# Attention with a graph dilation beside it: small numbers on GpSimd, one comparison moved between two products, second projections in another bank, and joined statistics

## The chip, the core and the metric

The kernel runs on one core of a Trainium2 chip. The metric is the device time of one launch in microseconds: 3422.03 us before the change, the median of three runs (3410.63 to 3422.94). The profiled execution took 3413.46 us, of which 3411.7 us lie between its first and its last instruction.

In the profile PE is TensorE's matmuls, PEld its weight loads, DVE VectorE, ACT ScalarE, POOL GpSimd and SP SyncE. Times are microseconds unless marked ns.

## What is computed

There are 16 graphs with 1024 nodes each and 128 features per node. Two layers follow each other.

```python
h = relu(layernorm(x))
x = x + attention(h, adj)          # 8 heads of 16, masked where adj == 0, weighted by adj
h = relu(layernorm(x))
x = x + sage(h, dilate(adj))       # three SAGE layers with batch norms, a projection at the end

# attention, per graph and head
scores = q @ k.T / sqrt(16);  scores[adj == 0] = -inf
attn = softmax(scores) * adj;  attn = attn / (attn.sum(-1) + 1e-8);  ctx = attn @ v

# dilate, per graph: rows in their order, each row sees what earlier rows removed
for n in range(1024):
    num = row.sum()
    sf = (num + 1) // 2 if num > 10 else 1
    removed = row & (cumsum(row) % sf == 0)      # if num > 1
    row n and column n lose what is removed
```

A row with more than ten neighbours loses the neighbour whose rank is sf and the one whose rank is twice sf; a row with two to ten loses all. The dilation needs only the adjacency, so it can run beside the attention.

## The kernel before

`swept` has two stages. The first (`first_part`) runs the attention of all graphs, the layer norms and, beside them, the dilation. The second runs the three SAGE layers. The change touches the first stage alone.

**The attention** (`attention`, L527) goes through 256 turns: graph b, half c of the query columns (512 of them), block m of 128 keys. Each turn has two half-steps, g = 0 and 1, with four heads each. A half-step gives VectorE, ScalarE and TensorE this work:

- `scores` (L586): 16 small bf16 matmuls that put a large negative number where there is no edge (L601), then the products of q and k (L609), into two PSUM tiles `sc` of two banks each.
- Two exponentials on ScalarE (L643), each over 128x1024: tiles `e`.
- Two products on VectorE (L658): `w` is `e` times the transposed adjacency `aT`, 128x1024 f32 each. These are the two weighted exponentials.
- `values` (L531): the sums with v (L534, from `w`) and the denominators' part (L539, from `e`), issued one half-step late.
- Once per turn, `turn_over` (L544): TensorE transposes the adjacency block two turns ahead into PSUM bank `m` (L552), ScalarE evicts it (L555) and makes the mask (L559), and SP sends it away.

**What is woven in.** Preparations of the next graph (`prepare`: layer norm, transposes, projections to q, k and v), conclusions of the last one (`conclude`) and the like are generators. They lie in the list `beside`; at marked places of a half-step `go_on_with(kind)` lets one whose last yield named that kind go on. `both_groups` (L352) is the generator of the q and k projections: for each of two groups a matmul of 512 columns into a PSUM tile (L356), an eviction by ScalarE (L337, L345) and a second one by VectorE that keeps the low part (L339, L347). All four of a graph's projections use the one PSUM bank `m` for both groups (graph 0's first two alternate with bank `d`). So the second group's matmul comes after VectorE has read the first, and when the second group is still to be read, `held` is true (L632) and the transposes of `turn_over`, which need bank `m` too, are issued later.

**The layer norms** (`layer_norm_relu`, L288) take `bn_stats` per block of 128 nodes (L294: for each half of the features count, mean and count times variance), join the two halves with `bn_aggr` (L296), raise the variance to the power -1/2 on GpSimd (L302) and let ScalarE apply scale and bias (L308). There are 32 of them over eight blocks, the first in two parts.

**The dilation** (`dilation`, L708) goes through eight blocks k of 128 rows, all 16 graphs at once, rows on partitions. Per block:

1. VectorE builds prefix sums `w` of the diagonal blocks by scans (L813) and the masks `up`, `valid`, `final`. The small numbers of 128x16 (`onw`, `total`, `most`, `half`, `end16`, L831 to L843) say how many neighbours a row has and where its middle is.
2. Seven rounds (L863 on) find a fixed point. A round takes `gone`, what the other rows removed, from PSUM bank `d`. From it come `num` and `y`, then `c`, `high` and `at16` (L880, L881, L884), all of 128x16. Then `hit` compares the 128x2048 prefix sums with `at16` (L893), and TensorE counts the hits per row into `gone` (L899, 16 matmuls of one column). Rounds in the set `full` also make `vb` (L887 to L891) and 32 more matmuls (L903, L904). `full` has two of the seven rounds in blocks 0 to 4, four in block 5, and all in blocks 6 and 7: 28 of 56.
3. The last numbers (L911 to L922), the removal from the diagonal blocks (L925 to L937), then 18 iterations over the graphs that apply the result to all columns: scan (L957), transposes (L964), evictions (L966), comparisons (L973 to L992) and the reading of the next block.

**What sets the order.** `beside_attention` (L1006) is a planner written out by hand. `dilation` is a generator that yields a cost in us and when it wants to go on: 0 at once, 1 after the next half-step, "A" or "B" at the next half-step of that parity. After each half-step the planner takes steps of the dilation while the costs spent lie below a share of the total that grows with the half-steps; the total is made of the cost of a block, in which a round counts 2.5. A yield marked "counts" makes the planner issue the scores of the next half-step before the dilation goes on, so that the matmuls of `gone` stand behind these scores in TensorE's queue. Rounds 1 and 3 wait one half-step between the small numbers and `hit`.

```python
                    yield (1.6 if r in full else 1.0), (1 if r in (1, 3) else 0)
                    nc.vector.tensor_tensor(in_pairs(hit), in_pairs(w), over_rows(at16), ALU.is_equal)
                    yield 1.3, 1, "counts"
```

Each engine works through its instructions in the order in which they are issued here, with small moves by a scheduler. GpSimd's queue holds little before the change: the powers of the layer norms (L302), casts of reciprocals (L457), the fill of `go_on` (L803), and DMAs.

## Time and profile before

| | PE | PEld | DVE | ACT | POOL |
|---|---|---|---|---|---|
| busy us | 3238.2 | 1904.3 | 3050.6 | 2350.6 | 165.4 |
| share of the span | 95% | 56% | 89% | 69% | 5% |
| instructions | 34987 | 34987 | 5410 | 3942 | 253 |

| costliest rows of the first stage | count | busy us | mean ns |
|---|---|---|---|
| L658 DVE, products `w` | 1024 | 1210.7 | 1219 |
| L643 ACT, exponentials `e` | 1024 | 997.6 | 1022 |
| L534 PE, sums with v | 4096 | 605.2 | 608 |
| L539 PE, denominators | 4096 | 587.1 | 593 |
| L609 PE, scores | 4096 | 378.9 | 444 |

The profiled execution took 3413.46 us and its span is 3411.7 us; 1.8 us lie around it. Busy time is a union of intervals from start to end of each instruction; instructions that follow each other on an engine overlap a little, so the distance from start to start is the better price. PE's ends are modelled, and a busy PE isn't PE at its peak. The chain that ended last holds only the last two VectorE instructions in this trace, so what bounds the kernel has to be read from stretches, groups and timelines. A wait is given with what ended it ("<-ACT e L643").

### The profile page before, as it was taken

The page shows a single profiled execution, that of the slowest core. Times are in us where ns is not written, and L with a number is a line of the kernel's source. Part 1 is how long each engine was busy: PE and PEld are TensorE (multiplying, and loading weights), DVE is VectorE, ACT ScalarE, POOL GpSimd, SP SyncE. Part 2 cuts the span into 40 slices and gives each one's busy share as a digit, 9 for nine tenths or more (in the row PEclk, how much of TensorE's full clock was granted, in tenths as well). Part 3 has the DMA queues.
Part 4 walks back from the last instruction along what each step waited for, and adds up shares of the span by engine and source line. Part 5 has one row for each costly group of instructions (what it writes and reads, how often), then busy time and mean ns, then how long its engine had stood idle before and what let it go on. Part 6 is the DMA issues. An engine that isn't in the chain of part 4 may idle for free. (4 is left out here: it accounts for less than half of the span.)

```text
span 3411.7 us, 86821 instructions
## 1 busy us (share of the span) xinstructions
PE 3238.2 (95%) x34987; PEld 1904.3 (56%) x34987; DVE 3050.6 (89%) x5410; ACT 2350.6 (69%) x3942; POOL 165.4 (5%) x253
## 2 busy tenths in 40 slices
PE   8999999999999999999899999999999899999997
PEld 3433333333343333333334334346999899999997
DVE  7988988998999898998999999997888799988887
ACT  7699789779879979978987996994322344433324
POOL 2000000000000000000000010001000000000000
PEclk9999999999999999999999999999999999999999
DMA  7356456547646746754864783577999799989996
GB/s 237 108 168 197 138 147 204 153 133 214 183 127 200 226 125 181 236 152 146 240 190 127 221 256 105 167 241 268 347 343 341 284 350 351 349 326 350 352 348 223
DMA packets 650126, 772.31 MB, mean 226 GB/s; under 512 B 173264, under 2 KB 569168, under 8 KB 637424
## 3 DMA queue, kind: packets, MB, share of 16 engines
q1 hardware_dynamic: 632672, 708.58, 64.1%
q0 software_dynamic: 15456, 57.30, 4.8%
q8 instruction: 276, 4.52, 0.6%
q14 instruction: 138, 1.13, 0.1%
q10 hardware_dynamic: 1584, 0.79, 0.1%
HBM read 508.50 MB, written 157.29 MB: 195 GB/s over the span
## 5 line engine op out<-in xcount | busy, mean ns | idle before, releaser
L658 DVE TENSOR_TENSOR w<-e,aT 128x1024 f32<-128x1024 f32 x1024 | 1210.7, 1219 | 139.6 <-ACT e L643 138.0
L643 ACT ACTIVATE e<-sc 128x1024 f32<-128x1024 f32 x1024 | 997.6, 1022 | 194.1 <-PE sc L609 193.0
L1196 PE MATMUL pg<-y,aT 128*128 128x128 f32 (+1 forms) x6144 | 730.6, 275 | 0.0
L1196 PEld LDWEIGHTS pg<-y,aT 128*128 128x128 f32 x6144 | 708.7, 192 | 0.0
L534 PE MATMUL acc<-w,both 128*32 128x512 f32 x4096 | 605.2, 608 | 3.5 <-DVE w L658 1.9
L539 PE MATMUL acc<-e,eps 128*32 128x512 f32 x4096 | 587.1, 593 | 0.0
L147 DVE SCALAR_TENSOR_TENSOR aT<-mr,aT 128x1024 f32<-128x1024 bf16 x384 | 458.8, 1217 | 0.0
L609 PE MATMUL sc<-q,k 32*128 32x512 f32 x4096 | 378.9, 444 | 0.0
L601 PE MATMUL sc<-nomask,never 32*32 32x512 bf16 x8192 | 287.8, 384 | 70.2 <-ACT e L643 62.9
L601 PEld LDWEIGHTS <-never 32*32 32x32 bf16 x8192 | 91.3, 87 | 412.9 <-issue 392.7
L539 PEld LDWEIGHTS acc<-e,eps 128*32 128x32 f32 x4096 | 152.4, 110 | 298.3 <-issue 291.2
L1219 ACT ACTIVATE sq<-o 128x512 f32<-128x512 f32 x96 | 60.6, 631 | 328.4 <-DVE o L1214 328.4
L1237 ACT COPY hT<-pt 128x512 f32<-128x512 f32 x96 | 56.2, 585 | 288.5 <-PE pt L1233 280.0
L609 PEld LDWEIGHTS sc<-q,k 32*128 32x128 f32 x4096 | 155.3, 183 | 150.1 <-issue 150.0
L973 ACT ACTIVATE pair<-both,th 128x512 f16<-128x512 f16 x256 | 205.4, 881 | 2.0 <-DVE both L957 2.0
L552 PE MATMUL pa<-ident,a 128*128 128x128 f32 x1024 | 168.3, 287 | 35.1 <-DVE q L339 15.4
L534 PEld LDWEIGHTS acc<-w,both 128*32 128x32 f32 x4096 | 94.8, 108 | 181.1 <-DVE w L658 80.9
L552 PEld LDWEIGHTS pa<-ident,a 128*128 128x128 f32 x1024 | 107.6, 141 | 151.8 <-issue 61.4
L555 ACT COPY aT<-pa 128x512 f32<-128x512 f32 x256 | 152.5, 596 | 52.0 <-PE pa L552 51.4
L559 ACT ACTIVATE nomask<-aT 128x512 bf16<-128x512 f32 x256 | 161.5, 631 | 8.1
L1214 DVE SCALAR_TENSOR_TENSOR o<-pg,rdeg,mine 128x128 f32<-128x128 f32 x384 | 108.1, 344 | 56.7 <-PE pg L1196 53.5
L957 DVE TENSOR_TENSOR_SCAN both<-rk 128x513 f16<-128x513 bf16 x128 | 156.0, 1218 | 0.0
(240 smaller groups left out, 4058.2 us busy)
## 6 DMA issues: line engine op xcount, KB each, us to landing
aT<-aT_d SPq DMA_DIRECT2D x94, 2048.0 KB, 10.0
mr<-mr_d SPq DMA_DIRECT2D x188, 512.0 KB, 6.0
aT_d<-aT SPq DMA_DIRECT2D x256, 256.0 KB, 4.1
a<-in_adj SPq DMA_DIRECT2D x253, 256.0 KB, 3.4
ad<-in_adj SPq DMA_DIRECT2D x112, 512.0 KB, 4.5
nomask<-nomask SPq DMA_DIRECT2D x512, 96.0 KB, 2.7
nomask<-nomask SPq DMA_DIRECT2D x512, 64.0 KB, 2.7
nomask<-nomask SPq DMA_DIRECT2D x512, 32.0 KB, 2.6
```

The lines of the kernel that those rows point to most:

```text
L147: nc.vector.scalar_tensor_tensor(part, mrs[h][:, j : j + 2, :].rearrange("p j n -> p (j n)"), 0.0, part, ALU.is_equal, ALU.mult)
L534: nc.tensor.matmul(acc[g][32 * j : 32 * j + 32, :], v1[:, m, (2 * j + g) * HW : (2 * j + g) * HW + 32], ws[j // 2][:, j % 2, :], start=(m ...
L539: nc.tensor.matmul(acc[g][32 * j : 32 * j + 32, :], eps8, es[j // 2][:, j % 2, :], start=False, stop=(m == NB - 1),)
L552: nc.tensor.transpose(pa[:, k * P : (k + 1) * P], a[:, k, :], ident)
L559: nc.scalar.activation(nomask[:, 0, :], aT[:, 0, :], AF.Relu, bias=1.0, scale=-1e38, accum_out=zeros[:, i : i + 1])
L601: nc.tensor.matmul(scs[j // 2][to : to + 32, j % 2, :], never[rows, rows], nomask[rows, j, :], start=True, stop=False, tile_position=(32 * ...
L609: nc.tensor.matmul(scs[j // 2][:, j % 2, :], ks[m // HB][rows, g, mm], qs[c][rows, g, half, :], start=False, stop=(half == 1), tile_positi ...
L643: nc.scalar.activation(e, scs[q], AF.Exp, scale=1.0 / math.sqrt(HD))
L658: nc.vector.tensor_tensor(w, es[q], aT.to_broadcast([P, 2, HN]), ALU.mult)
L957: nc.vector.tensor_tensor_scan(pair_sums[b % 2], row[:, 0::2], row[:, 1::2], 0.0, ALU.add, ALU.add)
L973: nc.scalar.activation(wrs[b][:, t::2], pair_sums[b % 2][:, t : t + HN], AF.Abs, bias=at[:, b : b + 1], scale=2.0,)
L1196: nc.tensor.matmul(pg[:, i // 2, at : at + width], aT[:, j, i * P : (i + 1) * P], y[:, j, :width], start=(j == 0), stop=(j == NB - 1),)
```

## The change

It has four parts.

1. **Joined statistics.** `bn_aggr` goes. Six VectorE instructions on all blocks at once join the halves: difference of the means, sum of the variances, the square of the difference scaled, their sum, the scaling with epsilon, the sum of the means.
2. **Second projections in the dilation's bank.** A flag `taken["d"]` says whether a tile of bank `d` is still to be read by VectorE in the written order. If not, the second group of a projection goes to bank `d`, else to `m` as before. `held` is true only if it went to `m`.
3. **Small numbers on GpSimd.** In `dilation` the 128x16 instructions that don't read PSUM are issued on GpSimd. Where VectorE did two operations with two tensors in one instruction, GpSimd gets two instructions. `num`, `y`, `mosts` and `mids` of rounds 1 to 6 read `gone` in PSUM and stay on VectorE.
4. **The comparison between the two products.** A round's `hit` is not issued in `dilation` but put in the list `amid`, and the next half-step issues it between its two products `w`. A round yields once instead of twice, so each round takes one half-step. In the planner a round counts 1.9 instead of 2.5.

```diff
@@ layer_norm_relu
-                for j in range(i, i + 2):
-                    nc.vector.bn_aggr(mv[:, j, :], st[:, j, :])
...
-            nc.vector.tensor_scalar(rs[:, 1, n], mv[:, n, 1], LN_EPS, None, ALU.add)
+            apart, squares = mv[:, n, 0], mv[:, n, 1]
+            nc.vector.tensor_tensor(apart, st[:, n, 1], st[:, n, 4], ALU.subtract)
+            nc.vector.tensor_tensor(squares, st[:, n, 2], st[:, n, 5], ALU.add)
+            nc.vector.scalar_tensor_tensor(apart, apart, D / 4.0, apart, ALU.mult, ALU.mult)
+            nc.vector.tensor_tensor(squares, squares, apart, ALU.add)
+            nc.vector.tensor_scalar(rs[:, 1, n], squares, 1.0 / D, LN_EPS, ALU.mult, ALU.add)
+            nc.vector.tensor_tensor(apart, st[:, n, 1], st[:, n, 4], ALU.add)
             nc.gpsimd.tensor_tensor(rs[:, 0, n], rs[:, 1, n], minus_half[:, n], ALU.pow)
...
@@ both_groups
                     where, tag = banks[g % len(banks)]
+                    if g == 1 and len(banks) == 1:
+                        if not taken["d"]:
+                            where, tag = ps_d, "d"
+                        taken["m"] = tag == "m"
@@ attention
-                    held = go_on_with("next step")
+                    held = go_on_with("next step") and taken["m"]
...
                         ws.append(w)
+                        while q == 0 and amid:
+                            amid.pop()()
                         if q == 0:
                             go_on_with("low")
@@ dilation, before the rounds
-                        nc.vector.tensor_scalar(onw, w[:, :, P - 1], 1024.0, None, ALU.subtract)
+                        nc.gpsimd.tensor_scalar(onw, w[:, :, P - 1], 1024.0, None, ALU.subtract)
...
-                        nc.vector.tensor_tensor(total, left, right, ALU.add)
+                        nc.gpsimd.tensor_tensor(total, left, right, ALU.add)
...
+                    taken["d"] = True
                     yield (2.5 if c == 0 else 1.4), 1
                     nc.vector.tensor_tensor(valid[:, hb, :], pd, up[:, hb, :], ALU.mult)
+                    taken["d"] = False
...
@@ dilation, a round
+                    taken["d"] = False
                     if r == ROUNDS - 1:
-                        nc.vector.tensor_copy(prev, num)
-                    nc.vector.tensor_scalar(c, y, MAGIC, MAGIC - 5120.0, ALU.add, ALU.subtract)
-                    nc.vector.tensor_scalar(high, num, 10.5, None, ALU.is_gt)
+                        nc.gpsimd.tensor_copy(prev, num)
+                    nc.gpsimd.tensor_scalar(c, y, MAGIC, MAGIC - 5120.0, ALU.add, ALU.subtract)
+                    nc.gpsimd.tensor_scalar(high, num, 10.5, -4096.0, ALU.is_gt, ALU.mult)
...
-                    nc.vector.scalar_tensor_tensor(at16, twice(high), -4096.0, twice(c), ALU.mult, ALU.add)
+                    nc.gpsimd.tensor_tensor(at16, twice(high), twice(c), ALU.add)
                     if r in full:
...
-                        nc.vector.scalar_tensor_tensor(
-                            vb[:, 0], twice(num), 1.5, twice(high), ALU.is_gt, ALU.subtract
-                        )
-                        nc.vector.scalar_tensor_tensor(c, y, 5120.0, c, ALU.add, ALU.is_gt)
-                        nc.vector.tensor_tensor(vb[:, 1], twice(c), twice(high), ALU.mult)
-                    yield (1.6 if r in full else 1.0), (1 if r in (1, 3) else 0)
-                    nc.vector.tensor_tensor(in_pairs(hit), in_pairs(w), over_rows(at16), ALU.is_equal)
-                    yield 1.3, 1, "counts"
+                        nc.gpsimd.tensor_scalar(high, num, 10.5, None, ALU.is_gt)
+                        nc.gpsimd.tensor_scalar(lost, num, 1.5, None, ALU.is_gt)
+                        nc.gpsimd.tensor_tensor(vb[:, 0], twice(lost), twice(high), ALU.subtract)
+                        nc.gpsimd.tensor_tensor(c, y, c, ALU.subtract)
+                        nc.gpsimd.tensor_scalar(c, c, -5120.0, None, ALU.is_gt)
+                        nc.gpsimd.tensor_tensor(vb[:, 1], twice(c), twice(high), ALU.mult)
+                    amid.append(
+                        partial(nc.vector.tensor_tensor, in_pairs(hit), in_pairs(w), over_rows(at16), ALU.is_equal)
+                    )
+                    taken["d"] = True
+                    yield (2.0 if r in full else 1.7), 1, "counts"
+                    while amid:
+                        amid.pop()()
...
@@ dilation, after the rounds
                 nc.vector.tensor_tensor(changed[:, k * B : (k + 1) * B], num, prev, ALU.not_equal)
-                nc.vector.tensor_scalar(high, num, 10.5, None, ALU.is_gt)
-                nc.vector.scalar_tensor_tensor(allof, num, 1.5, high, ALU.is_gt, ALU.subtract)
+                nc.gpsimd.tensor_scalar(high, num, 10.5, None, ALU.is_gt)
+                nc.gpsimd.tensor_scalar(allof, num, 1.5, None, ALU.is_gt)
+                nc.gpsimd.tensor_tensor(allof, allof, high, ALU.subtract)
...
@@ beside_attention
-            block = 1.3 + 4.6 + 3.9 + 1.4 + 1.2 + 2.6 + ROUNDS * 2.5 + 2.0 + 5.1 + 1.4 + B * 4.2 + 2.4
+            block = 1.3 + 4.6 + 3.9 + 1.4 + 1.2 + 2.6 + ROUNDS * 1.9 + 2.0 + 5.1 + 1.4 + B * 4.2 + 2.4
```

Seven more instructions between L914 and L922 move to GpSimd in the same way, as do the four copies ahead of the first round (L860, L861, L869, L870).

## The prediction, made before the changed kernel was run

> **What bounds the kernel now.** I read the busy shares by stretch first, because the span has two stages. Up to about 2330 us the attention runs with the dilation beside it; the rest is SAGE. Columns: stretch, its length, then busy us of PE, PEld, DVE, ACT, POOL, then clock and DMA.
>
> ```profile
> 30.00:2330.00 2300.00, 2175.84 (x25775) 864.99 (x25774) 2115.61 (x3495) 1959.44 (x3128) 108.30 (x140) 1.00 0.59 178
> 2330.00:3411.70 1081.70, 1042.88 (x9119) 1029.92 (x9110) 918.09 (x1850) 374.72 (x783) 46.27 (x86) 0.98 0.91 329
> ```
>
> The diff touches only the first stage, 512 half-steps (one group g of one block m). There VectorE is busy 2115.6 of 2300 us (92%), PE 95% by modelled ends. Which of the two paces? The timeline of PE shows a half-step in which nothing waits:
>
> ```profile
> 1223.43 0.43 PE L601 MATMUL sc<-nomask,never 32*32 32x512 bf16 x16
> ...
> 1226.91 0.43 PE L601 MATMUL sc<-nomask,never 32*32 32x512 bf16 x16
> ```
>
> So 3.48 us is PE's own pace; the average is 2300/512, about 4.5 us. What fills a half-step beyond 3.48 is VectorE: two products L658 (1.14 us from start to start) and what stands between them. The groups name VectorE's largest row, its only large wait, and the small PE waits which the second projections cause:
>
> ```profile
> L658 DVE TENSOR_TENSOR w<-e,aT 128x1024 f32<-128x1024 f32 x1024 | 1210.7, 1219 | 139.6 <-ACT e L643 138.0
> ...
> L552 PE MATMUL pa<-ident,a 128*128 128x128 f32 x1024 | 168.3, 287 | 35.1 <-DVE q L339 15.4 <-DVE k L347 12.1 <-DMA a<-in_adj 5.9
> ...
> L893 DVE TENSOR_TENSOR hit<-w,at 128x2048 bf16<-128x2048 f16 x56 | 68.3, 1219 | 0.5
> ```
>
> So VectorE is the nearer bound, and time taken from it counts almost fully. Now the rounds, from the timeline of VectorE:
>
> ```profile
> 1229.15 0.17 DVE L876 TENSOR_TENSOR v<-parts,gone 128x16 f32<-128x16 f32 x1
> 1229.23 0.17 DVE L877 SCALAR_TENSOR_TENSOR v<-gone,parts 128x16 f32<-128x16 f32 x1
> 1229.43 0.17 DVE L880 TENSOR_SCALAR v<-v 128x16 f32<-128x16 f32 x1
> 1229.52 0.17 DVE L881 TENSOR_SCALAR v<-v 128x16 f32<-128x16 f32 x1
> 1229.72 0.19 DVE L884 SCALAR_TENSOR_TENSOR at<-v 128x32 f16<-128x32 f32 x1
> ```
>
> The reader is to see the prices: 0.08 us from start to start when the next instruction does not depend on this one, 0.20 when it does. The three small numbers of a round hold VectorE about 0.5 us, no more. That is what the change can win per round.
>
> **What the change puts in its place.** In a round VectorE now runs: first product w0, `hit`, second product w1, then num and y; GpSimd makes c, high and at16; the next half-step's w0; then `hit`, which waits for at16. In the written order w0 follows y directly. y takes 0.17 us but lets the next instruction start after about 0.12, so w0 runs before GpSimd can hear of y. Does that matter? The trace of before has the same situation: the power on GpSimd (L302) waits for a small VectorE result (L301).
>
> ```profile
> 1201.13 1.64 POOL L302 TENSOR_TENSOR rs_a<-rs_a,minus_half 128x8 f32<-128x8 f32 x1 [36.00 <-DVE rs_a L301]
> ```
> ```profile
> 379.44 0.17 DVE L301 TENSOR_SCALAR rs_b<-mv_b 128x8 f32<-128x8 f32 x1
> 379.52 1.22 DVE L854 TENSOR_TENSOR final<-w,end 128x2048 bf16<-128x2048 f16 x1
> ```
> ```profile
> 379.70 2.54 POOL L302 TENSOR_TENSOR rs_b<-rs_b,minus_half 128x8 f32<-128x8 f32 x1 [33.23 <-DVE rs_b L301]
> ```
>
> The first power ran beside instructions with one SBUF tensor and took 1.64 us. The second started 0.18 us into a VectorE product of two SBUF tensors and took 2.54: 0.90 longer, to the end of that product. At 909.68 it stood behind a scan of 2.29 us and took 3.54. So a GpSimd instruction that reads SBUF stands still while such a VectorE instruction, already begun, runs. w0 is one (e times aT), `hit` and w1 too. The chain therefore begins when w0 lets go, about 1.07 us after its start, and VectorE has then nothing to do but wait for at16. The work is moved off VectorE, and the wait for it is put back on VectorE.
>
> The Trainium skill, "SBUF — State Buffer", section Who interferes with whom, states more than these rows show: the second to issue fully blocks until the first is done, for every instruction. By it a chain that is still running beside `hit` and w1 is stopped anew at each; without that, the full round below would lose about 0.5 us less, or 14 us in all.
>
> **Price of one small GpSimd instruction.** No row of before has these operations. Lowest reading row: the cast of `rden` (L457, 128x16), 0.197 us. Highest: the power takes 1.034 us for 4 elements and 1.64 for 8, so 0.15 per element and 0.43 with none. I take 0.22 for one input and 0.30 for two, near the cast, since the operations are plain; 0.08 for a hand-over (L301's end to L302's start). Ends kept: 0.20 and 0.43. The skill's "GPSIMD Engine Reference", section Elementwise — side-by-side cycle accounting, gives 4497 ns for 2048 elements, by which 16 elements would cost an estimated 35 ns beyond a fixed part that it leaves open; the sum would be that of the lower end.
>
> **The sum.** (1) *Rounds.* The eight stretches from a block's first `hit` to its seventh:
>
> ```profile
> sum 282.90, PE 277.74 PEld 128.34 DVE 268.49 ACT 197.10 POOL 10.12; mean PE 34.72 PEld 16.04 DVE 33.56 ACT 24.64 POOL 1.27
> ```
>
> Each holds 8 half-steps now and 6 after, one per round. A plain round after: `hit`, w1 and w0 3 x 1.14, num and y 0.20, wait 0.80 (1.07 + 0.22 + 0.22 + 0.30 + 0.08 less 1.14, rounded up), other VectorE work and gaps of an average half-step 0.45 (what the 268.5 + 14.4 us leave over products, hits and small numbers): 4.85 us. A full round (c, high also shape vb; 28 of 56) has one to two more instructions ahead of at16 (wait 1.0) and five behind it. Two of these get through between `hit` and w1; the rest, 0.75, run after w1, then 32 matmuls at 25 ns apart (0.8) and 0.4 of hand-overs: VectorE waits 1.95 for `gone`, and mosts, mids, num and y take 0.5. That is 6.85, with 0.25 of other work that isn't covered 7.1. PE waits too: `gone` is queued ahead of the value matmuls. Blocks 0 to 4 have one full interval of six, block 5 three, blocks 6 and 7 six: 5 x 31.35 + 35.85 + 2 x 42.6 = 277.8. The last round of each block is full and its wait now falls on VectorE: 8 x 1.95 = 15.6. The 16 half-steps set free still have to be run, near PE's pace: 16 x 3.6 = 57.6. Together 351 against 282.9: **+68**. At 0.20 per instruction this is +46, at 0.43 +113.
> (2) *Small numbers outside the rounds* (L831, L836 to L843, the four copies, L914 to L922): 0.08 + 1.16 + 0.31 + 1.28 = 2.83 us per block by start times, used half-steps later, so hidden on GpSimd: 22.6, at 92% **-20**.
> (3) *Statistics*: per layer norm eight aggregations (0.15 each, two in 0.30) and two small instructions go, seven small ones come, most dependent: 1.36 against about 1.15, 32 times: **-5** (0 to -8).
> (4) *Second projections*: PE waits now 15.4 + 7.4 + 12.1 + 5.0 = 40 us for q and k to be read (L552 and L356). Following the flags through the written order, 49 of 62 take the other bank, and the transposes are no longer held. VectorE has its own 139.6 us of waiting for e, part of it behind these: I take half, **-20** (-40 to +10: the other bank can itself be read late).
> (5) About one power per block falls between two rounds ahead of the chain: **+3**.
> No DMA issue changes its queue or its number. Sum +26 us (0.8%). On the profiled execution's 3413.5 that is 3440; the median of the runs, 3422.0, lies 8.6 higher, so 3448 on it. I take **3443**.
>
> **The rivals.** *A, faster: the block does not reach the chain*, because a half-step's w0 is late (waits for e) or short reads pass beside it. Then 3 instructions end within w0's 1.07 us; it decides when each is under 0.33. Plain round 4.1, full 4.85 (vb is late by 0.5): 212 + 4 + 57.6 = 273.5, so -9, and with the rest -20 - 5 - 20 = -54: 3359 to 3368, say 3364. For it: the 138 us of waits for e. Against: in the rounds VectorE is 95% busy, and both powers above. *B, dearer:* each instruction 0.43: +113 - 42 = +71, some 3489. Against it: the cast row. *C, about equal:* 0.20 each: +46 - 42 = +4, some 3422; for it the cast row, against it that most instructions here wait for the one before. *D*, that the other bank brings nothing, is +20 on the forecast and within B's end.
>
> **Numbers.** Forecast 0.44, A 0.25, B 0.14, C 0.17. A measurement can tell 0.5% (17 us) from no change: slower by more is 0.38 of the forecast, all of B and 0.02 of C, 0.54; within 0.06 and 0.13, 0.19; faster A and 0.02 of C, 0.27. The range spans A to B: 3366 to 3487. The slower cases alone span 3425 to 3487.
>
> **What would show it.** `hit` gets a wait of 0.8 to 1.2 us for GpSimd; num (and mosts in full rounds) one of about 2 us for `gone`; the rounds' stretches are about 35 to 43 us for six half-steps; GpSimd's c or high starts at w0's end and not beside it. If `hit` follows w0 without idle time, the forecast is wrong and A holds. If idle time ahead of L658 near q and k stays as it is, term 4 is wrong.

## The result and the profile after

The changed kernel takes 3473.99 us (median of four runs, 3471.68 to 3479.04) where the kernel before takes 3422.49 in the same runs: 1.0157 times as long, 95% interval 1.0139 to 1.0174, or 51.5 us more. The forecast was 3443, 31 us less. The profiled execution took 3471.68 us with a span of 3469.8.

The busy time by stretch, with the same columns as before the change. The first stage now ends near 2391 us, not 2330; SAGE keeps its length.

```profile
30.00:2391.00 2361.00, 2215.40 (x25791) 877.11 (x25787) 2062.02 (x2988) 1960.95 (x3128) 391.77 (x660) 0.97 0.58 173
2391.00:3469.80 1078.80, 1039.61 (x9103) 1026.69 (x9099) 917.05 (x1846) 374.72 (x783) 46.38 (x86) 0.99 0.91 329
```

VectorE has less work (2062.0 us, before 2115.6), and its stage is 61 us longer: its idle time grew from 184 to 299 us. The clock column fell from 1.00 to 0.97, which the prediction did not speak of. The groups of VectorE and TensorE in the changed kernel say what VectorE waits for:

```profile
L669 DVE TENSOR_TENSOR w<-e,aT 128x1024 f32<-128x1024 f32 x1024 | 1215.0, 1219 | 161.0 <-ACT e L654 159.4
L672 DVE TENSOR_TENSOR hit<-w,at 128x2048 bf16<-128x2048 f16 x56 | 68.5, 1224 | 37.5 <-POOL at L900 37.1
L889 DVE TENSOR_TENSOR parts<-cs,gone 128x16 f32<-128x16 f32 x20 | 3.4, 171 | 31.9 <-PE gone L925 31.9
...
L563 PE MATMUL pa<-ident,a 128*128 128x128 f32 x1024 | 168.8, 288 | 8.3 <-DMA a<-in_adj 5.9
...
L990 PE MATMUL pe<-ident_bf,pair 128*128 128x128 bf16 x1024 | 79.1, 220 | 15.4 <-DVE q L344 10.7 <-DVE k L352 2.5 <-DVE pair L1011 1.9
```

Three waits grew. `hit` waits 37.1 us for `at16` (0.5 in whole before). The counts behind full rounds cost 31.9 us at `mosts` (L889; 4.0 before), and 14.1 more after each block's last round (1.5 before). The products wait 159.4 for `e` (138.0 before). TensorE's waits for q and k ahead of the transposes of `turn_over` (27.5 us of 35.1) are down to 1.7. But the dilation's own transposes (L990), which use bank `d` too, now wait 13.2 us for q and k where they waited for neither before, so half of that part's gain on TensorE has only moved.

One plain round, from the timelines of VectorE and then of GpSimd:

```profile
1227.44 0.16 DVE L892 SCALAR_TENSOR_TENSOR v<-gone,parts 128x16 f32<-128x16 f32 x1
1227.53 1.21 DVE L669 TENSOR_TENSOR w<-e,aT 128x1024 f32<-128x1024 f32 x1
1229.61 1.23 DVE L672 TENSOR_TENSOR hit<-w,at 128x2048 bf16<-128x2048 f16 x1 [0.87 <-POOL at L900]
```
```profile
1227.61 1.27 POOL L897 TENSOR_SCALAR v<-v 128x16 f32<-128x16 f32 x1 [22.37 <-DVE v L892]
1228.96 0.29 POOL L896 TENSOR_SCALAR v<-v 128x16 f32<-128x16 f32 x1
1229.33 0.24 POOL L900 TENSOR_TENSOR at<-v 128x32 f16<-128x32 f32 x1
```

The product starts 0.08 us ahead of the chain's first operation, which then takes 1.27 us instead of 0.29 and ends when the product does. That a GpSimd operation stands still while a product runs that began before it is called the lock below. The other two run while VectorE has nothing to do. In a full round the chain goes on, and it stops again at `hit` and at the second product. GpSimd, then TensorE:

```profile
1237.16 1.30 POOL L903 TENSOR_SCALAR v<-v 128x16 f32<-128x16 f32 x1
1238.53 1.01 POOL L906 TENSOR_TENSOR v<-v 128x16 f32<-128x16 f32 x1
1239.51 0.24 POOL L905 TENSOR_TENSOR vb<-v 128x32 bf16<-128x32 f32 x1
1239.83 0.25 POOL L907 TENSOR_SCALAR v<-v 128x16 f32<-128x16 f32 x1
1240.16 0.25 POOL L908 TENSOR_TENSOR vb<-v 128x32 bf16<-128x32 f32 x1
```
```profile
1238.38 0.55 PE L920 MATMUL gone<-one_bf,hit 128*128 128x1 bf16 x16 [1.08 <-DVE hit L672]
1239.80 0.16 PE L924 MATMUL gone<-vb,valid 128*128 128x1 bf16 x1 [0.86 <-POOL vb L905]
1240.46 0.16 PE L925 MATMUL gone<-vb,final 128*128 128x1 bf16 x1 [0.50 <-POOL vb L908]
```

So TensorE stands still three times in one round, with the value matmuls of the attention queued behind. VectorE gets `gone` at 1241.41, after 1.85 us of waiting.

Not every round is like these two. In the trace, 48 rounds follow another one. In 23 of them the first operation of the chain is stopped by a product, and `hit` waits 0.86 to 1.46 us. In 14 it is a later operation, and the wait is 0.14 to 0.84. In 8 none is stopped before `at16` is made, and `hit` waits for nothing. In the other 3 the power of a layer norm (L307, 1.67 us) stands on GpSimd ahead of the chain, and `hit` waits 1.19 to 1.48; the full round above is one of these, though rounds like it whose first operation is stopped wait as long (1.18).

### The profile page after: what moved, and what is told of

It is laid out like the page before. It is cut to its first block, busy times and chain, and to the rows that moved or that the text cites. A ratio compares the mean times of both kernels' runs of the same rounds, so it can differ in the third digit from the quotient of the medians.

```text
span 3469.8 us, 86966 instructions
## 1 busy us (share of the span) xinstructions
PE 3274.7 (94%) x34987; PEld 1913.3 (55%) x34987; DVE 2996.2 (86%) x4899; ACT 2352.2 (68%) x3942; POOL 449.0 (13%) x773
## 5 line engine op out<-in xcount | busy, mean ns | idle before, releaser
L669 DVE TENSOR_TENSOR w<-e,aT 128x1024 f32<-128x1024 f32 x1024 | 1215.0, 1219 | 161.0 <-ACT e L654 159.4
L654 ACT ACTIVATE e<-sc 128x1024 f32<-128x1024 f32 x1024 | 998.5, 1023 | 216.3 <-PE sc L620 215.9
L545 PE MATMUL acc<-w,both 128*32 128x512 f32 x4096 | 619.6, 626 | 6.1 <-DVE w L669 4.7
L550 PE MATMUL acc<-e,eps 128*32 128x512 f32 x4096 | 595.6, 606 | 0.0
L983 DVE TENSOR_TENSOR_SCAN both<-rk 128x513 f16<-128x513 bf16 x128 | 156.1, 1220 | 0.0
```

The source lines that it names most:

```text
L545: nc.tensor.matmul(acc[g][32 * j : 32 * j + 32, :], v1[:, m, (2 * j + g) * HW : (2 * j + g) * HW + 32], ws[j // 2][:, j % 2, :], start=(m ...
L550: nc.tensor.matmul(acc[g][32 * j : 32 * j + 32, :], eps8, es[j // 2][:, j % 2, :], start=False, stop=(m == NB - 1),)
L654: nc.scalar.activation(e, scs[q], AF.Exp, scale=1.0 / math.sqrt(HD))
L669: nc.vector.tensor_tensor(w, es[q], aT.to_broadcast([P, 2, HN]), ALU.mult)
L983: nc.vector.tensor_tensor_scan(pair_sums[b % 2], row[:, 0::2], row[:, 1::2], 0.0, ALU.add, ALU.add)
```

## The experiments

My theory after the result: the loss is the chain on GpSimd, by VectorE's wait in front of `hit` and by the late `vb`. Rivals: the new place of `hit` with the planner's 1.9; the second projections; GpSimd's mere presence; TensorE's lower clock. Each ratio below is to runs of the kernel before on the same chip, whose medians were 3415.7 to 3418.3 us.

| kernel | median us | ratio, 95% interval |
|---|---|---|
| e1, all numbers on VectorE | 3420.16 | 1.001 (0.9999 to 1.002) |
| e2, rounds' numbers on VectorE | 3416.44 | 0.9995 (0.9985 to 1.0004) |
| e3, bank alone | 3409.39 | 0.9977 (0.9968 to 0.9986) |
| e4, statistics alone | 3415.89 | 0.9998 (0.9988 to 1.0009) |
| e5, comparison first | 3475.49 | 1.0172 (1.0155 to 1.0189) |
| e6, TensorE filled ahead of the count | 3479.84 | 1.0176 (1.0157 to 1.0195) |
| e7, GpSimd part alone | 3479.68 | 1.0185 (1.0163 to 1.0207) |
| e8, without the moved comparison | 3477.27 | 1.0181 (1.0162 to 1.02) |
| e9, `vb` on VectorE | 3437.91 | 1.006 (1.0043 to 1.0078) |
| e10, `at16` on VectorE | 3433.73 | 1.0047 (1.0031 to 1.0063) |
| e11, a second chain nobody reads | 3422.02 | 1.0017 (1.0007 to 1.0028) |
| e12, bank and numbers outside | 3402.66 | 0.996 (0.9946 to 0.9975) |
| e13, numbers outside alone | 3406.07 | 0.9963 (0.9949 to 0.9978) |
| e14, moved comparison alone | 3429.45 | 1.0036 (1.002 to 1.0051) |
| e15, TensorE filled behind the count | 3467.87 | 1.0144 (1.0123 to 1.0165) |

**e1 and e2: the numbers back on VectorE.** e1 undoes all of part 3 in the changed kernel, e2 only its round:

```diff
-                    nc.gpsimd.tensor_scalar(c, y, MAGIC, MAGIC - 5120.0, ALU.add, ALU.subtract)
+                    nc.vector.tensor_scalar(c, y, MAGIC, MAGIC - 5120.0, ALU.add, ALU.subtract)
...
-                        nc.gpsimd.tensor_tensor(vb[:, 0], twice(lost), twice(high), ALU.subtract)
...
+                        nc.vector.scalar_tensor_tensor(
+                            vb[:, 0], twice(num), 1.5, twice(high), ALU.is_gt, ALU.subtract
+                        )
```

> The changed kernel with every small number of the dilation back on VectorE; the joined statistics, the second projections in the dilation's bank, the comparison between the two weighted exponentials and the planner's 1.9 per round stay. Theory 1 (the loss is the chain on GpSimd: VectorE's 37.1 us in front of `hit`, and the rounds' PE idle that goes with it): no wait of `hit` for GpSimd is left, the eight rounds' stretches (first to seventh `hit`) come back to about 283 us or below, half-clock windows of PE fall from some 36 to under 12, and the time is 3380 to 3425 us, before or a little under it. Rival 2 (the place of `hit` and the planner's smaller cost per round are the cause, since they move 24 half-steps out of the rounds and behind them): it stays at 3455 to 3480. Rival 3 (the second projections cost, through the scores that wait for them): the same as rival 2, and the experiment with that part alone is slower than before.

> The changed kernel with only the rounds' numbers (previous count, c, high, at16, and the full rounds' vb) back on VectorE; those of the diagonal products, the two copies ahead of the first round and those behind the last round stay on GpSimd. Theory 1 (the loss is made by the serial chain inside a round, and the numbers outside the rounds save VectorE about 20 us): under the all-VectorE version by 0 to 20 us, 3360 to 3420. A rival, that any GpSimd work beside VectorE's exclusive operations costs as much as it saves: equal to the all-VectorE version or up to 15 us above it. The rival that the place of `hit` is the cause: 3440 to 3470.

Both times lie in the ranges of theory 1. From e2 to the changed kernel it is 1.0157 against 0.9995: 1.62%, some 55 us, for the rounds' numbers alone. The half-steps, counted as two products each, lie the same way in both (48 in the rounds' stretches, 68 from the last `hit` to the first scan). The rounds' stretches are 35 us shorter in e2 (256.4 in all, against 291.6, which is shown further down), and from the last `hit` to the first scan it is 20 us less: the whole difference lies there. That sum and the groups of VectorE in e2:

```profile
sum 256.39, PE 232.91 PEld 111.10 DVE 233.63 ACT 151.26 POOL 7.84; mean PE 29.11 PEld 13.89 DVE 29.20 ACT 18.91 POOL 0.98
```
```profile
L669 DVE TENSOR_TENSOR w<-e,aT 128x1024 f32<-128x1024 f32 x1024 | 1215.3, 1219 | 148.0 <-ACT e L654 146.4
L672 DVE TENSOR_TENSOR hit<-w,at 128x2048 bf16<-128x2048 f16 x56 | 68.2, 1218 | 0.0
L889 DVE TENSOR_TENSOR parts<-cs,gone 128x16 f32<-128x16 f32 x20 | 3.4, 171 | 13.2 <-PE gone L924 13.2
```

Against the changed kernel `hit` saves 37 us, the counts 19 and, behind the last rounds, 13, the products 13: 82 us of waiting; VectorE works 30 us more (2091.7 in its first stage against 2062.0). The difference, 52, is about the 55.

**e3 and e4: one part each, on the kernel before.** e3 takes the hunks of `both_groups`, `held` and `taken` from the diff above, e4 those of `layer_norm_relu`.

> The kernel before with one part of the change: the second projections go to the dilation's bank while it is free, and a step's first turn-over is held only where they took the other bank. Theory 1 (PE's 35.1 us of waiting for the second projections' bank was worth about 20 us on the path): 3395 to 3412. The rival that another wait (the exponentials' wait for scores) takes its place: 3417 to 3428. The rival that it costs, since the bank is held when the dilation wants it: 3430 to 3450.

> The kernel before with one part of the change: the two halves' statistics are joined for all tiles of a group at once. My estimate was 5 us less: 3412 to 3422. The rival, that these operations lie beside waits of VectorE anyway: 3420 to 3426.

The bank brought 0.23%, 8 us, where theory 1 counted on about 20; the statistics brought nothing that can be measured. Where the rest of the bank's gain went, the groups of TensorE and ScalarE in e3 say:

```profile
L648 ACT ACTIVATE e<-sc 128x1024 f32<-128x1024 f32 x1024 | 998.2, 1022 | 216.6 <-PE sc L614 216.3
L557 PE MATMUL pa<-ident,a 128*128 128x128 f32 x1024 | 168.3, 287 | 11.8 <-DMA a<-in_adj 6.0 <-DVE q L339 2.7 <-DVE k L347 2.3
L560 ACT COPY aT<-pa 128x512 f32<-128x512 f32 x256 | 152.8, 597 | 14.2 <-PE pa L557 13.8 <-issue 0.4
L976 PE MATMUL pe<-ident_bf,pair 128*128 128x128 bf16 x1024 | 79.2, 220 | 13.3 <-DVE q L339 6.5 <-DVE k L347 3.9 <-DVE pair L997 2.8
```

The wait ahead of the transposes fell from 35.1 to 11.8 us, and ScalarE's behind them from 52.0 to 14.2. But the dilation's transposes (L976) now wait 10.4 us for q and k, and ScalarE waits 216.3 us for scores (193.0 before). VectorE's wait for `e` fell only from 138.0 to 130.8, and its low parts of q and k wait 14 us for ScalarE instead of 5.

**e5: the comparison ahead of both products.**

```diff
+                    while amid:
+                        amid.pop()()
                     for q in range(2):
                         w = pool.tile([P, 2, HN], F32, name=f"w_{b}_{c}_{m}_{g}_{q}", tag="w", bufs=4)
                         nc.vector.tensor_tensor(w, es[q], aT.to_broadcast([P, 2, HN]), ALU.mult)
                         ws.append(w)
-                        while q == 0 and amid:
-                            amid.pop()()
```

> The changed kernel with the round's comparison issued ahead of both weighted exponentials of the half-step, not between them. Theory (the chain is slowed by the first of them, which shuts GpSimd out, and the late count of `gone` follows from the late comparison): GpSimd's first operation of the chain takes 0.29 us in nearly all rounds, not 1.27; `hit` waits 1.2 to 1.6 us per round for a whole chain of 0.35 us per operation, where it waited 0.9 behind a product; VectorE's waits for `gone` (31.9 us at the halving of the next round) fall under 10, since two products lie behind the comparison: 48 rounds x (0.5 - 1.0 to 1.5) = 25 to 50 us less, 3425 to 3455. A rival (GpSimd's operations are slow by themselves or by its own queue): the waits of `hit` are 2 us and more, and the time 3465 to 3500.

The first operation is free as expected, but there is no gain: 3475 us is the rival's time, though the rival's sign, waits of `hit` of 2 us and more, isn't there. GpSimd's groups in e5:

```profile
L903 POOL TENSOR_SCALAR v<-v 128x16 f32<-128x16 f32 x28 | 32.9, 1176 | 2.5
L905 POOL TENSOR_TENSOR vb<-v 128x32 bf16<-128x32 f32 x28 | 29.2, 1042 | 0.0
...
L897 POOL TENSOR_SCALAR v<-v 128x16 f32<-128x16 f32 x56 | 18.4, 328 | 190.0 <-DVE v L892 188.6
```

The first operation has a mean of 328 ns (649 in the changed kernel), so the lock's place was read rightly. But `hit` waits 51.5 us for the whole chain (0.9 for each of 56, under the 1.2 to 1.6 expected), and the counts still 32.1, where under 10 was expected: what delays them is not the late `hit` but the late `vb` (e9 below takes it away), whose operations now run into `hit` and two products (L903, L905 and L906 are long in 25, 23 and 27 of 28).

**e7 and e8: the comparison where it stood.** e7 is part 3 alone on the kernel before; e8 is the changed kernel without part 4.

> The kernel before with one part of the change: all small numbers of the dilation on GpSimd; the comparison stands where it stood, one slot of the attention's work behind the numbers, the planner's cost of a round is 2.5, statistics and banks as before. Theory 1 (the loss needs the chain directly in front of the comparison): a half-step's work lies between the numbers and `hit`, the chain is over in time, `hit` waits under 0.3 us, and the time is 3385 to 3425. Rival (operations of GpSimd cost wherever they stand, by shutting VectorE out or by being late): 3440 to 3480.

> The changed kernel with the comparison and the planner's cost of a round as in the kernel before; the numbers on GpSimd, the second projections in the dilation's bank and the joined statistics stay. Theory 1: the run with the numbers on GpSimd alone, less the 7 us that the bank gave: 3378 to 3418. Rival (GpSimd's operations cost wherever they stand): 3433 to 3473.

Theory 1 of these two texts fell: the loss doesn't need the moved comparison. I had taken for granted that a half-step lies between numbers and `hit`; in the code it does so only in rounds 1 and 3. VectorE's timeline in e7, first a `hit` of round 3, then one of round 4:

```profile
1282.00 1.22 DVE L899 TENSOR_TENSOR hit<-w,at 128x2048 bf16<-128x2048 f16 x1
...
1288.23 0.17 DVE L881 SCALAR_TENSOR_TENSOR v<-gone,parts 128x16 f32<-128x16 f32 x1
1289.42 1.23 DVE L899 TENSOR_TENSOR hit<-w,at 128x2048 bf16<-128x2048 f16 x1 [1.02 <-POOL at L889]
```

The 16 `hit` with a half-step in front wait 5.4 us in all, 0.3 each; the 8 of the first rounds wait for nothing; the other 32 wait 43 us, 1.3 each, for a chain that takes VectorE about 0.5. So a half-step in front takes most of the wait away. A half-step in front of every `hit` was not tried: by the yields of the written order a block takes some 62 half-steps, and with 40 more in all the eight blocks don't end within the 512 that the attention has.

**e9 and e10: one half of the round's numbers each.** In e9 VectorE makes `vb` behind `hit`, in e10 it makes `c`, `high` and `at16`.

```diff
+                        def bits(num=num, y=y, c=c, lost=lost, vb=vb):
+                            nc.vector.tensor_scalar(lost, num, 10.5, None, ALU.is_gt)
...
+                        amid.insert(0, bits)
```
```diff
-                    nc.gpsimd.tensor_tensor(at16, twice(high), twice(c), ALU.add)
+                    nc.vector.scalar_tensor_tensor(at16, twice(high), -4096.0, twice(c), ALU.mult, ALU.add)
```

> The changed kernel with the two factors of the full rounds (vb, 28 of the 56 rounds) computed by VectorE behind the comparison, in four operations; the previous count, c, high and at16 stay on GpSimd. Theory, as the runs so far leave it (VectorE loses by two waits: 37.1 us for at16 in front of the comparison, and some 31 us more than the all-VectorE version for the counts behind full rounds, because GpSimd's factors come late): the counts' wait falls from 51 to about 20 us, the wait of `hit` stays at 35 to 40, VectorE works some 12 us more: 3445 to 3465. Rival (one wait only matters, the comparison's): no change, 3470 to 3485.

> The counterpart: the previous count, c, high and at16 on VectorE, the factors of the full rounds on GpSimd. Theory: the wait of `hit` goes (37 to under 2), the counts' wait stays near 30 to 50 us in whole, VectorE works some 22 us more: 3425 to 3450, and the two halves' losses against the version with all the rounds' numbers on VectorE (3416) add up to about the 57 us of both. Rival (the factors are hidden behind the comparison and the products): 3412 to 3422.

Each takes away more than half: 0.97% and 1.10% of the 1.57%. The gains add up to 71 us, not 55; put as losses against e2, the two halves cost 22 and 18 us, 40 together, where the text of e10 expected about 57. So the two waits overlap, and each fix alone also brings the wait for `e` back (159.4 to about 147 and 150). The groups of VectorE, e9 first:

```profile
L672 DVE TENSOR_TENSOR hit<-w,at 128x2048 bf16<-128x2048 f16 x56 | 68.6, 1224 | 31.7 <-POOL at L900 30.6
L889 DVE TENSOR_TENSOR parts<-cs,gone 128x16 f32<-128x16 f32 x20 | 3.3, 165 | 16.3 <-PE gone L929 16.3
```
```profile
L672 DVE TENSOR_TENSOR hit<-w,at 128x2048 bf16<-128x2048 f16 x56 | 69.3, 1237 | 0.0
L889 DVE TENSOR_TENSOR parts<-cs,gone 128x16 f32<-128x16 f32 x20 | 3.4, 171 | 24.5 <-PE gone L924 24.5
```

e9 was 7 us better than its expected range: not only the counts' wait fell but also those of `hit` and of the products.

**e11: a chain that nobody waits for.** e2, and the round's numbers once more on GpSimd into tiles of their own:

```diff
+                    nc.gpsimd.tensor_scalar(sc, y, MAGIC, MAGIC - 5120.0, ALU.add, ALU.subtract)
+                    nc.gpsimd.tensor_scalar(shigh, num, 10.5, -4096.0, ALU.is_gt, ALU.mult)
+                    nc.gpsimd.tensor_tensor(sat, twice(shigh), twice(sc), ALU.add)
```

> The version with the rounds' numbers on VectorE, and beside it the same numbers once more on GpSimd, into tiles that nobody reads (what is used is computed as before). It has GpSimd's work of the changed kernel in the rounds without anybody's wait for it. Theory (the loss is waiting, not GpSimd's presence): 3411 to 3423, with the first small operation behind a product again at 1.2 us and VectorE's products at 1.22 us as ever. Rival (GpSimd's operations slow VectorE or its queue by sharing the memory's port): 3435 and more, and VectorE's products longer.

1.0017 against 0.9995 of e2: 0.22%, about 8 us of the 55 (3 to 12 by the two intervals) come with GpSimd's presence; the rest comes only when something waits for the chain. VectorE's products kept their 1220 ns.

**e12, e13 and e14: the other parts.** e13 is the kernel before with part 3 outside the rounds, e12 adds the bank to it, e14 is the kernel before with part 4 alone.

> The kernel before with the two parts that did not cost: second projections in the dilation's bank while it is free, and the small numbers outside the rounds (diagonal products, copies ahead of the first round, those behind the last) on GpSimd; the rounds' own numbers on VectorE, comparison, planner and statistics as before. By the runs of the parts (7 us from the bank; 4 us from the numbers outside) 3400 to 3410 where the kernel before has 3416. A rival: those behind the last round lie in front of the products that use them, so that they cost what they save: 3407 to 3415.

> The kernel before with one part of the change in part: the small numbers outside the rounds on GpSimd, nothing else. My prediction's term was 20 us less, 0.6% (3396 where the kernel before has 3416). What the two differences of the runs so far say: 4 to 6 us less, 0.1 to 0.2% (3410 to 3412), because freed time of VectorE comes back in part as a longer wait for the exponentials (about half of 20 us).

> The kernel before with one part of the change: the comparison is issued between the next half-step's two products and a round counts 1.9 in the planner, so that a round takes one half-step; all small numbers on VectorE, banks and statistics as before. By subtraction from the runs so far it should cost 8 to 14 us, 0.25 to 0.4% (3424 to 3430 where the kernel before has 3416): `hit` never waits, but the counts' wait behind full rounds grows from 4 to 13 us. Rival: it costs nothing by itself, and the 10 us are interplay with the bank: 3413 to 3420.

The moved comparison costs 12 us by itself; its rival, no cost, fell. In its profile the rounds' stretches shrink by 26 us and the time from the last `hit` to the first scan by 11, but the 20 half-steps that leave these stretches (16 and 4) come back as 53 us elsewhere, 2.6 each. The counts behind full rounds wait 11.2 us (4.0 before). The numbers outside gave 12.6 us (7.5 to 17.4), more than the 4 to 6 I had by subtraction, less than the 20 predicted. Stretch and group of e13:

```profile
30.00:2322.00 2292.00, 2168.40 (x25755) 866.14 (x25752) 2094.55 (x3334) 1958.83 (x3127) 221.99 (x316) 1.00 0.60 179
```
```profile
L658 DVE TENSOR_TENSOR w<-e,aT 128x1024 f32<-128x1024 f32 x1024 | 1211.0, 1219 | 153.5 <-ACT e L643 151.6
```

VectorE works 21 us less (2115.6 before) and waits 13.6 us more for `e`. Bank and numbers together (e12) give 14 us (8.5 to 18.4), where the two alone add up to 20; that they share a part of it is likely by these numbers, not shown. e12 is the fastest of all kernels here, 0.4% under the kernel before, though its interval doesn't part it from e13.

**e6 and e15: is it TensorE's clock?** In the first stage the clock was at half for 17 us before and for 120 us after, in windows of 3.41 us; after the change about 106 of the 120 lie in or right behind the rounds. Three neighbouring windows of the changed kernel (columns as above):

```profile
1237.70:1241.20 3.50, 1.45 (x47) 1.32 (x48) 1.86 (x3) 2.65 (x4) 2.46 (x5) 1.00 0.70 215
1241.20:1244.60 3.40, 3.40 (x23) 1.33 (x24) 2.66 (x8) 0.00 (x0) 0.96 (x4) 0.50 0.15 41
1244.60:1248.00 3.40, 3.40 (x60) 1.54 (x56) 2.68 (x5) 1.59 (x2) 0.77 (x2) 0.99 0.00 0
```

A window in which TensorE worked 1.45 us of 3.5, with pauses of 1.08, 0.86 and 0.50, is followed by one at half clock. Both experiments put matmuls that compute nothing into such pauses, e6 ahead of every count, e15 in full rounds behind the 16 counting matmuls:

```diff
+                        for _ in range(5):
+                            nc.tensor.matmul(gone[:, 128:512], upto, valid[:, 0:3, :], start=True, stop=True)
```

> The changed kernel with five matmuls that compute nothing that is used (128 x 384, into columns of the count's bank that nobody reads) ahead of every round's count, so that TensorE is busy while it waits for the comparison; results are as before. The rival to be tested is that the lower clock of TensorE (36 windows of 3.41 us at half in the changed kernel, 5 in the kernel before) makes most of the loss beyond the forecast: then the half-clock windows in the rounds go, and the time falls by 20 to 45 us, to 3430 to 3455. If the clock costs little, since TensorE waits in those windows anyway: 3468 to 3485 with fewer such windows, a little more where the five matmuls (about 0.8 to 1.4 us together) come late and push the count back.

> The changed kernel with five matmuls that compute nothing that is used (128 x 384, into columns of the count's bank that nobody reads), in full rounds only, behind the 16 counting matmuls and ahead of the 32 that wait for GpSimd's factors, 0.8 us where TensorE waits 1.4 us. If TensorE's half clock costs much: half-clock time in the first stage falls from 119 us to 80 or less, and the time by 10 us or more, to 3455 to 3464. If TensorE only waits there anyway: half-clock time falls and the time stays at 3470 to 3480. If half-clock time doesn't fall, idle time of 0.8 us less is not what sets it.

In e6 the half-clock time fell to 85 us, but the counts waited 13 us longer, so its time says nothing of the clock. In e15 it fell from 120 to 72 us, and the ratio from 1.0157 to 1.0144: 4 us, within both intervals, and a time between the two ranges expected. Here too the counts behind full rounds waited longer, 37.4 us against 31.9. The stretches of the rounds of blocks 0, 1, 5 and 6, the changed kernel and then e15:

```profile
102.15:134.85 32.70, 29.82 (x425) 13.77 (x421) 23.61 (x36) 16.77 (x25) 13.64 (x27) 0.90 0.34 104
382.67:415.69 33.02, 29.22 (x422) 13.08 (x416) 24.93 (x46) 19.89 (x33) 14.57 (x29) 0.90 0.32 97
1503.45:1542.16 38.71, 34.92 (x487) 14.96 (x485) 28.16 (x55) 20.61 (x30) 18.88 (x33) 0.91 0.24 73
1796.37:1839.16 42.79, 37.14 (x585) 17.51 (x581) 27.14 (x51) 19.94 (x30) 27.89 (x50) 0.92 0.21 64
```
```profile
101.31:131.96 30.65, 28.02 (x430) 13.78 (x426) 23.43 (x37) 16.76 (x25) 13.56 (x27) 1.00 0.37 112
379.82:411.86 32.04, 28.56 (x427) 13.40 (x421) 24.88 (x46) 19.89 (x33) 15.22 (x29) 0.95 0.32 99
1497.72:1536.69 38.97, 34.38 (x502) 15.66 (x500) 28.12 (x55) 20.60 (x30) 18.65 (x33) 1.00 0.24 72
1790.75:1835.81 45.06, 39.05 (x615) 19.59 (x611) 27.15 (x51) 19.93 (x30) 27.84 (x50) 1.00 0.20 60
```

In blocks 0 and 1, with one full round each between the first and the seventh `hit`, the clock rose and the stretches became 2.1 and 1.0 us shorter; in blocks 2 to 4 neither the clock nor the length changed by more than 0.01 and 0.4 us. In blocks 5 and 6, with three and six full rounds, a full clock (0.91 and 0.92 become 1.00) made them no shorter. There the added matmuls stand in half or all of the rounds, and what the clock gives can't be told from what they cost. So e15 leaves the clock's share open.

The runs of the kernel before say more, since each lists its span and mean clock, and the traces here know only full and half clock, so that the time at half follows. Over the 35 runs on one chip it lies between 41 and 89 us, and the time rises by 0.32 us for each us of it (correlation 0.71); over the 20 and the 15 runs on two others it rises by 0.37 and 0.29. Which of the two makes the other, these runs do not show. The runs of the changed kernel are at half clock for 141 us on average, those of e2 for 72. At 0.3 us each that is, as an estimate, some 20 of the 55 us. In e15 it would be 10 us less (109 us at half), and the longer counts take back 5.5, which fits the 4 measured. The lower clock comes with the waiting, since e2 has little of it, but it may well be a part of the way in which the chain costs its time.

The Trainium skill, "TensorE: Matmul & The Clock Gate", section HAM oscillation — how this bites in real kernels, counts half of the throttled time as lost. By that the 48 us fewer of e15 would have brought an estimated 24; the run shows 4, and the runs of the kernel before about 0.3 us for each us at half clock.

## Why the prediction went wrong

*The mechanism was right, though not in every round.* The lock, the chain that starts when the product lets go, the wait put back on VectorE, and the late `vb`, all are in the timelines. The lock stopped the chain ahead of `at16` in 37 of the 48 rounds. `hit` waits 0.87 in the plain round shown (0.80 predicted) and 1.19 in the full one (1.0); 1.85 for `gone` (1.95). An unblocked operation took 0.22 to 0.29 us; 0.22 was taken for one input and 0.30 for two, where it is 0.25 to 0.29 for one and 0.22 to 0.25 for two. So rivals A (the lock doesn't reach the chain; true in 8 rounds), B (0.43 each) and C (about equal) fell. e5, where the lock hardly reaches the first operation, was no faster. That a chain is stopped anew at each later product, as the prediction cited from "SBUF — State Buffer", section Who interferes with whom, the trace confirms: L903 takes 1.3 us beside `hit` in 23 of 28 rounds and 0.26 otherwise.

*Term 1, the rounds, +68: right in sum, and in part by luck.* e14's 12 us for the new place and 55 for the chain make 67. Its parts were less good:

```profile
sum 291.57, PE 258.69 PEld 116.42 DVE 207.15 ACT 153.58 POOL 145.70; mean PE 32.34 PEld 14.55 DVE 25.89 ACT 19.20 POOL 18.21
```

The eight stretches are 291.6 us long, not 277.8, although the waits in them were smaller than priced: `hit` 37.1 us in all (42 predicted, 28 x 0.8 + 20 x 1.0) and the counts behind full rounds 31.9 (39 predicted, 20 x 1.95). The wait behind the last rounds was 14.1 (15.6 predicted). 16 half-steps left the rounds as predicted, but 4 more left the stretch behind them, and each of the 20 costs 2.6 us elsewhere in e14, not 3.6: 53 in all (57.6 predicted). So what is too high and what is too low in the term nearly cancel. What else fills the stretches no run shows in full; the lower clock, which stands in no term, is a part by the estimate above.

*The step that failed* is the sentence "time taken from it counts almost fully", and with it terms 2, 3 and 4. They were to give 20, 5 and 20 us; alone they gave 12.6, nothing and 8, and numbers and bank together 14. The prediction's sum was +26 us; with 14 in place of 45 it is +57, where 51.5 were measured. (3443 was a choice 5 us below the 3448 of that sum, so that its distance to the result is 31.) In term 2 VectorE did get its 21 us back, but not at 92%: 13.6 of them returned as waits for `e`. A 92% busy engine whose only large wait is 138 us for the engine ahead of it in the chain (ScalarE's `e`) does not set the pace alone, and its time can't be counted at 92%. In term 4 the halving of 40 us was no reading at all: the trace of before does not show which of TensorE's waits reach VectorE, 8 us did, and 10 of the 40 came back as waits of the dilation's transposes in the other bank (L976). Rival D (the bank brings nothing, +20) came near this; no rival priced term 2 falling short.

Term 5 (+3): a power ran ahead of the chain in 4 of the 48 rounds, and in the 3 where nothing else delayed it `hit` waited 4.1 us in all; no run prices it apart. The prediction left the clock out; what that cost it is the estimate above, not shown by an experiment.

## What to carry to other kernels

Moving small dependent operations from a busy engine to an idle one gains only where the result has time to arrive: here 0.5 us of VectorE's own work per round (30 us in all) became 1.2 us of waiting for `at16` and the counts (69 us), while the same kind of move outside the rounds gained. Before a gain is booked, the freed time has to be followed to what is late next; on a kernel with three engines over 80% busy in a stage, more than half of it came back. Of several parts of a change, the ones that gain (here 14 us) should be timed apart from those that lose (here 12 and 55).

## What the hardware showed that was not expected

In the first stage of the changed kernel TensorE's granted clock fell to half 27 times, 24 of them right after a window of 3.41 us in which TensorE worked 0.33 to 0.63 of the time, though no single pause was longer than 2.3 us. It is no rule: 10 windows with shares from 0.43 to 0.63 were not followed by half clock. The section on the clock gate named above speaks of idle gaps longer than some 3.4 us; here shorter ones, often several in a window, were enough. A GpSimd operation of 128x16 costs about 0.35 us from start to start (0.08 to 0.09 of it between the end of one and the start of the next), against 0.08 to 0.20 on VectorE, and 1.0 to 1.3 us when a VectorE product of two SBUF tensors has begun before it.
